# Turned orders and group releases of four-part tiles in a sparse four-layer graph network kernel

## The chip, the cores and the metric

One core of a Trainium2 chip runs the kernel. The metric is the device time of one execution in microseconds (us), lower is better; the median of several executions is compared. Engines are named as in the profile: PE multiplies matrices (PEld loads its weights), DVE and ACT work on whole tiles, POOL issues the indirect gathers, SP issues the plain DMAs.

## The reference, cut to what matters

`N` is 4096 nodes, 128 features each; `adj` is a 4096 x 4096 matrix that is mostly zero and dense in its first rows and columns. Four layers, each with a residual:

```python
h = relu(layernorm(x)); x = x + h @ W_self.T + (adj @ h) @ W_neigh.T + b                     # layer 0
h = relu(layernorm(x)); T1 = adj @ h; T2 = 2 * adj @ T1 - h
x = x + h @ w[0] + T1 @ w[1] + T2 @ w[2] + bias                                              # layer 1
h = relu(layernorm(x)); H = h @ weight.T
Tau = adj.T * exp(leaky_relu(alpha_src[None, :] + alpha_dst[:, None]))
x = x + (adj.T * Tau / Tau.sum(1)) @ H                                                       # layer 2
h = relu(layernorm(x)); s = h @ msg_s.T; d = h @ msg_d.T
agg = einsum('ijd,ij->id', gelu(s[:, None] + d[None] + msg_b), adj)                          # layer 3
x = x + layernorm(gelu([h, agg] @ upd_w.T + upd_b) + h) * ln_w + ln_b
```

## The kernel before

**What is computed where.** The kernel reads the whole of `adj` once, finds its non-zero places on the way, and from then on works on dense blocks where `adj` is dense and on lists where it is not. A list entry is a row of a feature table that POOL gathers by an indirect DMA: 128 rows at a time, one row for each partition. All gathers go through one helper, so all have the line L553 in the profile; they are told apart by their tiles.

**Three propagations (class `Layer`).** They are `adj @ h` of layer 0, and `adj @ h` and `adj @ T1` of layer 1. The output is cut into 16 stripes of 256 columns. For each stripe PE adds up the near blocks (L1138, tiles `big`, loaded by SP) and then the list chunks (L1155). A chunk takes a gathered table row tile `g` (slots `rows_g`, 14 of them) and a segment of `adj`; layer 0 gathers the segment too (`rseg`, 8 slots) and keeps it in the DRAM table `r_tab`, the others load it from there, up to four chunks in one `big` tile. Each propagation has 68 chunks. In the kernel before, the slot of a `g` tile is given back after its own matmul (L1157).

**Attention (class `Attention`, layer 2).** Per stripe of 256 columns there are batches of up to four blocks or chunks. For a batch, ACT makes `e` (relu with the gathered `g` or resident `hB` as bias, L1228, one instruction a part; exp over the batch, L1231), DVE multiplies it with the segments twice (`tau`, L1235, and `e`, L1237), and PE adds up one row of sums (L1252) and 128 rows of features (L1254), one matmul a part. 74 chunks are gathered from `a_tab` into the same 14 slots. When a pair of stripes is through, `finish_3` normalises, transposes (L588), multiplies (L597) and stores four blocks of `d_tab` (SP, L1307).

**Messages (class `Messages`, layer 3).** 158 chunks of single entries. For each, POOL gathers rows of `d_tab` into one part of a tile `m` of four parts (`m0` to `m3`, and later halves of the old `e` and `tau` tiles, which keep these names in the profile), DVE builds one part of `r` (L1400), PE adds the rows (L1406, L1408), ACT applies gelu (L1412) and PE adds up (L1418). All but 21 of these chunks need the whole of `d_tab`, and so the end of the attention; the 21 of block 0 need its first stripes alone. The value of each entry is gathered too: 158 gathers `e_val`, which only the messages need and which are put between other gathers from 500 us on.

**What sets the order.** Every piece of work is a generator that yields what it wants next: an event, a slot of a pool, or time on an engine. A planner (`Plan.run`) records the instructions in the order in which its own costs let them begin, and `in_order` pins that order on every engine. `plan.release(slots, item, time)` puts a slot back with the time from which the planner holds it free; a task that wants a slot takes the one with the smallest (time, index). So a change in a release moves which slot a later gather gets, and when the planner lets it begin, and through that the order in POOL's queue. Where the planner sees PE idle, `fill` (L604 to L609) records matmuls of zeros.

Waits are not written by hand. The build gives an instruction a wait for each earlier use of its tiles that earlier waits of its engine do not already cover, and lets an instruction of PE raise PE's semaphore only if another instruction waits for just that one (the others are counted in with the next). Where an instruction needs several waits, the further ones stand before it in its queue as instructions of their own (EventSemaphore).

`to_features` (L582 to L592) turns four blocks of 128 rows into columns: ACT has written them one by one (L578), PE transposes each into a quarter of a bank (L588), ACT copies the bank.

Of the kernel before, what the change touches and what calls it, by code (L numbers as in the profile page):

```python
# [31 lines left out]
GB = BANK // D  # L32
# [338 lines left out]
def on_pe(n, count=1):  # L371
    return "PE", (0.12 + 2.15e-3 * n) * count
# [6 lines left out]
def sparse_stack(tc, x, adj, adjT, diag, w_self, w_neigh, b0, w1, b1, w2, att_src, att_dst,  # L379
# [8 lines left out]
    plan = Plan()  # L388
    EARLY = 7
    with ExitStack() as ctx:  # L390
# [4 lines left out]
        def tiles(pool, name, n, shape, dtype=F32):  # L395
            return Slots([pool.tile(list(shape), dtype, name=f"{name}{i}", tag=f"{name}{i}") for i in range(n)])
# [20 lines left out]
        banks = tiles(ps, "bank", 3, (P, BANK))  # L417
        picks = tiles(ps, "pick", 2, (P, BANK))
# [163 lines left out]
        def to_features(blocks, rows):  # L582

            n = blocks.stop - blocks.start
            p = yield banks
            yield "PE", 0.42 * n
            for k in range(n):
                nc.tensor.transpose(p[:, k * P:(k + 1) * P], rows[:, k, :], ident)  # L588
            yield on_act(n * P)
            nc.scalar.copy(hT[:, blocks.start * P:blocks.stop * P], p[:, :n * P])  # L590
            plan.release(banks, p)
# [11 lines left out]

        def fill(begin, time):  # L604

            idle = min((free, i, slots.items) for slots in (banks, picks) for free, i in slots.free + [(1e9, 0)])
            if idle[0] < begin - 1.0:
                for _ in range(int(time / 0.22)):
                    nc.tensor.matmul(idle[2][idle[1]], nothing[:, :P], nothing, start=True, stop=True)  # L609
# [455 lines left out]
        class Layer:  # L1065
# [58 lines left out]
            def multiply(self):  # L1124
                for g in range(NC):
                    bank = yield accs
                    for s in ROWS:
                        if s.lo // BANK != g:
                            continue
                        acc = bank[:, s.lo % BANK:s.lo % BANK + RS]  # L1130
                        count, every = 0, len(s.near) + s.cap
                        for i, blocks in enumerate(s.tiles(TOGETHER)):
                            yield self.near_here[s.index][i]
                            t = self.at["near", s.index, i]
                            for k, b in enumerate(blocks):
                                yield self.near_done[b // GB]
                                yield on_pe(RS)
                                nc.tensor.matmul(acc, self.near[:, b, :D], as_rows(t)[:, k, :], start=count == 0,  # L1138
                                                 stop=count == every - 1)
                                count += 1  # L1140
                            plan.release(bigs, t)
                        for i, chunks in enumerate(s.groups(TOGETHER)):
                            if self.number:
                                yield self.list_here[s.index][i]
                                t = self.at["list", s.index, i]
                            for k, c in enumerate(chunks):
                                yield self.rows_here[s.index][c]
                                row = self.at["row", s.index, c]
                                if self.number:
                                    r = as_rows(t)[:, k, :]  # L1150
                                else:
                                    r, here, left = self.at["seg", s.index, c]
                                    yield here
                                yield on_pe(RS)
                                nc.tensor.matmul(acc, row[:, :D], r, start=count == 0, stop=count == every - 1)  # L1155
                                count += 1
                                plan.release(rows_g, row)  # L1157
                                if not self.number:
                                    left.set(plan.finish)
                            if self.number:  # L1160
                                plan.release(bigs, t)
                    agg = yield aggs
                    yield on_act(BANK)
                    nc.scalar.copy(agg, bank)
                    plan.release(accs, bank)
                    plan.start(self.finish(g, agg), -5)
                self.through.set(plan.finish)
# [6 lines left out]
        class Attention:  # L1174
# [40 lines left out]
            def attend(self, s, a, here, blocks, chunks, rows):  # L1215
                n = len(blocks or chunks)
                yield dst_done[s.lo // BANK]
                e = yield es_
                parts = []
                for k in range(n):  # L1220
                    if blocks:
                        yield a_done[blocks[k] // GB]
                        h = hB[:, blocks[k], :]
                    else:
                        yield rows[k][1]
                        h = rows[k][0]
                    yield on_act(CS + 100)
                    nc.scalar.activation(e[:, k, :], dst[:, s.lo:s.lo + CS], AF.Relu, bias=h[:, D:D + 1])  # L1228
                    parts.append(h)
                yield on_act(n * CS, "exp")  # L1230
                nc.scalar.activation(e[:, :n, :], e[:, :n, :], AF.Exp, scale=0.8)  # L1231
                yield here
                tau = yield taus
                yield on_dve(n * CS)
                nc.vector.tensor_mul(tau[:, :n, :], e[:, :n, :], a[:, :n, :])  # L1235
                yield on_dve(n * CS)
                nc.vector.tensor_mul(e[:, :n, :], tau[:, :n, :], a[:, :n, :])  # L1237
                plan.release(bigs, a)
                if s.index not in self.accs:
                    self.accs[s.index] = None  # L1240
                    self.accs[s.index] = yield accs
                    self.count[s.index] = 0
                while self.accs[s.index] is None:
                    yield acc_here[s.index]
                acc_here[s.index].set(0.0)
                every = len(s.near) + s.cap
                acc = self.accs[s.index]
                yield "PE", 0.4 * (self.count[s.index] == 0) + 2 * n * 0.65
                if self.count[s.index] == 0:
                    open_bank(acc)  # L1250
                for k in range(n):
                    nc.tensor.matmul(acc[0:1, CS:2 * CS], parts[k][:, D + 1:], tau[:, k, :], start=False, stop=False)  # L1252
                for k in range(n):
                    nc.tensor.matmul(acc[:, :CS], parts[k][:, :D], e[:, k, :], start=False,  # L1254
                                     stop=self.count[s.index] == every - 1)
                    self.count[s.index] += 1
                plan.release(taus, tau)
                plan.release(es_, e)
                for g, _ in rows:
                    plan.release(rows_g, g)  # L1260
                if self.count[s.index] == every:
                    plan.start(finish_3(s, acc), -5)
                    self.through.set(plan.finish)
# [52 lines left out]
        class Messages:  # L1316
# [27 lines left out]
            def rows(self, u, chunks, m, here):  # L1344
                groups = -(-4 * u.cuts[-1] // BANK)
                for g in range(groups):
                    yield d_here[g]
                for q, k in enumerate(chunks):
                    yield GATHER
                    n = u.within(k)  # L1350
                    gather(m[:n, q, :], d_tab[:groups * BANK, :], e_col[:n, k:k + 1])
                    here[q].set(plan.transfer(P * D * 4))

            def prepare(self, g):
# [21 lines left out]
                nc.scalar.activation(own, own, AF.Gelu)  # L1376
                r = yield r_tiles
                yield on_dve(BANK)
                for k in range(GB):
                    nc.vector.tensor_scalar(r[:, k, :], ident, diag_sb[:, g * GB + k:g * GB + k + 1], None, op0=ALU.mult)  # L1380
                self.acc[g] = acc = yield (accs if g else picks)
                yield "PE", 4 * 0.42
# [8 lines left out]
            def message(self, g, b, u, c, chunks, m, here):  # L1391
                n = len(chunks)
# [3 lines left out]
                yield self.s_here[g]  # L1396
                r = yield r_tiles
                yield "DVE", 0.35 * n
                for q, k in enumerate(chunks):
                    nc.vector.tensor_scalar(r[:, q, :], iota_row[:, :P], e_row[:, k:k + 1], e_val[:, k:k + 1],  # L1400
                                            op0=ALU.is_equal, op1=ALU.mult)
                for q in range(n):
# [91 lines left out]
        rows_g = tiles(main, "g", 14, (P, D + 2))  # L1494
# [55 lines left out]
        for i in range(2):  # L1550
# [6 lines left out]
            n = max(sum(u.cap for u in g.units) for g in GROUPS)  # L1557
# [429 lines left out]
```

## Time and profile before

| | |
|---|---|
| median of 8 runs | 1194.75 us (1189.5 to 1199.63) |
| the profiled execution | 1198.8 us, its span 1196.7 us |
| PE busy | 982.5 us, 82%, mean granted clock 0.927 |
| DVE / ACT / POOL busy | 793.9 / 672.4 / 772.4 us (66 / 56 / 65%) |
| DMA moved | 236.03 MB, mean 197 GB/s |
| gathers on POOL (L553) | 736: 68 `rseg`, 3 x 68 and 74 `g`, 74 `cseg`, 158 `e_val`, 158 of `d_tab` |
| matmuls of zeros (L609) | 795 |

PE's busy share holds the matmuls of zeros, so it does not say how much PE is needed. POOL's busy time is that of the gather instructions alone; the timeline has to be read to see at what pace they can follow each other. In lists of instructions the number in brackets is the idle time of the engine before the instruction, and what ended it. The chain of work that ended last is spread over all engines: PE 32%, DMA 28%, DVE 11%, POOL 10%, ACT 9%, issue 9%.

### The profile page before, as it was taken

What the parts mean: (1) busy time and instruction counts of PE and PEld (TensorE: products, weight loads), DVE (VectorE), ACT (ScalarE), POOL (GpSimd) and SP (SyncE); (2) the same over time, 40 slices, a digit from 0 to 9 for tenths busy, and PEclk for the clock granted to TensorE, in tenths of its full rate; (3) what the DMA queues carried; (4) which work ended last, traced back from release to release, by engine and by line L of the source; (5) the groups of instructions that cost most, each with busy time, mean ns of one, the idle gap of its engine ahead of it and who ended that gap; (6) DMA issues with size and microseconds to landing.
All of it is one profiled execution on the core that took longest, in us unless ns stands there. A gap on an engine that the chain in (4) does not pass through costs nothing.

```text
span 1196.7 us, 19187 instructions
## 1 busy us (share of the span) xinstructions
PE 982.5 (82%) x5943; PEld 672.7 (56%) x5943; DVE 793.9 (66%) x2982; ACT 672.4 (56%) x1344; POOL 772.4 (65%) x832
## 2 busy tenths in 40 slices
PE   5877988888888878778889788999999997879860
PEld 2545665555546656567667544454545665657650
DVE  5789987778878868667678665554546643356652
ACT  4997666676523221233456675686869742455771
POOL 5115777435656777777777777777777747777720
PEclk9989988879989999998899999999989999999995
DMA  7999999989748878889766533343444312223210
GB/s 225 364 329 352 388 367 394 369 305 353 262 141 268 253 222 278 249 282 288 211 192 188 171 91 106 115 116 113 111 129 122 92 51 60 52 68 86 69 36 21
DMA packets 175415, 236.03 MB, mean 197 GB/s; under 512 B 22452, under 2 KB 155336, under 8 KB 167112
## 3 DMA queue, kind: packets, MB, share of 16 engines
q1 hardware_dynamic: 148904, 186.45, 46.1%
q0 software_dynamic: 26400, 48.27, 15.7%
q8 instruction: 49, 0.80, 0.3%
q14 instruction: 62, 0.51, 0.1%
HBM read 203.41 MB, written 31.23 MB: 196 GB/s over the span
## 4 chain that ended last, share of the span: by engine, by line
PE 32%; DMA 28%; DVE 11%; POOL 10%; ACT 9%; issue 9%; SPq 1%; POOLq 0%; ACTq 0%; DVEq 0%
DMA g<-h_tab,fetch_row 5%; PE acc L1138 4%; POOL e_val L553 4%; PE acc L1155 4%; PE acc L1252 3%; PE acc L1254 3%; PE pick L609 3%; DMA big<-in_adjT 3%; DMA cseg<-in_adj,seg_col 3%; POOL g L553 3%; PE bank L609 3%; DMA dst<-in_adj 2%; PE bank L597 2%; DMA big<-r_tab 2%; DMA g<-a_tab,fetch_col 2%
## 5 line engine op out<-in xcount | busy, mean ns | idle before, releaser
L553 POOL DMA_INDIRECT e_val<-in_adj,e_at x158 | 160.0, 1013 | 48.0 <-issue 39.5
L553 POOL DMA_INDIRECT g<-h_tab,fetch_row x136 | 134.5, 989 | 45.4 <-issue 27.3
L609 PE MATMUL pick<-nothing 128*128 128x512 f16 x532 | 138.7, 409 | 0.0
L609 PEld LDWEIGHTS <-nothing 128*128 128x128 f16 x795 | 81.6, 105 | 90.8 <-issue 22.4
L1138 PE MATMUL acc<-big,hA 128*128 128x256 f32 x448 | 121.8, 418 | 12.8 <-DMA big<-in_adjT 10.0
L553 POOL DMA_INDIRECT rseg<-in_adjT,seg_row x68 | 70.7, 1039 | 77.3 <-issue 43.5
L1138 PEld LDWEIGHTS acc<-big,hA 128*128 128x128 f32 x448 | 89.7, 209 | 27.4 <-DMA big<-in_adjT 11.1
L768 ACT ACTIVATE mask<-dst 128x2048 fp8e4<-128x2048 f32 x43 | 81.9, 1905 | 25.7 <-DMA dst<-in_adj 25.5
L553 POOL DMA_INDIRECT cseg<-in_adj,seg_col x74 | 71.4, 965 | 36.6 <-issue 17.3
L553 POOL DMA_INDIRECT g<-a_tab,fetch_col x74 | 76.9, 1039 | 22.6 <-issue 13.1
L553 POOL DMA_INDIRECT m<-d_tab,e_col x70 | 68.5, 979 | 21.3 <-issue 11.6
L553 POOL DMA_INDIRECT tau<-d_tab,e_col x63 | 61.9, 983 | 30.2 <-DMA d_tab<-agg 11.3
L1155 PE MATMUL acc<-big,g 128*128 128x256 f32 x272 | 72.5, 399 | 10.2 <-DMA big<-r_tab 6.2
L1235 DVE TENSOR_TENSOR tau<-e,big 128x512 f32<-128x512 f32 (+3 forms) x61 | 54.3, 890 | 37.4 <-ACT e L1231 35.3
L553 POOL DMA_INDIRECT g<-u_tab,fetch_row x68 | 64.7, 952 | 20.7 <-issue 12.5
L568 ACT ACTIVATE junk<-xN,stat 128x128 f32<-128x128 f32 x128 | 51.3, 401 | 39.0 <-DVE stat L564 27.1
L1138 PE MATMUL acc<-big,hB 128*128 128x256 f32 x224 | 61.6, 412 | 13.4 <-DMA big<-in_adjT 13.4
L887 ACT COPY ehit<-pick 128x192 f32<-128x192 f32 (+7 forms) x74 | 20.2, 288 | 86.4 <-PE pick L884 73.3
L609 PE MATMUL bank<-nothing 128*128 128x512 f16 x263 | 66.7, 395 | 0.0
L1155 PEld LDWEIGHTS acc<-big,g 128*128 128x128 f32 x272 | 50.3, 197 | 21.7 <-issue 7.7
L890 DVE SCALAR_TENSOR_TENSOR ehit<-ehit,pos,pick 128x32 f32<-128x32 f32 (+7 forms) x158 | 38.7, 285 | 35.0 <-ACT ehit L887 34.7
L1155 PE MATMUL acc<-rseg,g 128*128 128x256 f32 x136 | 46.7, 451 | 16.6 <-DMA g<-h_tab,fetch_row 16.6
(328 smaller groups left out, 2582.0 us busy)
## 6 DMA issues: line engine op xcount, KB each, us to landing
dst<-in_adj SPq DMA_DIRECT2D x43, 1024.0 KB
big<-in_adjT SPq DMA_DIRECT2D x45, 512.0 KB
raw<-in_adj SPq DMA_DIRECT2D x21, 1024.0 KB
big<-in_adjT SPq DMA_DIRECT2D x66, 256.0 KB
big<-r_tab SPq DMA_DIRECT2D x30, 512.0 KB
c_tab<-cseg SPq DMA_DIRECT2D x74, 128.0 KB
r_tab<-rseg SPq DMA_DIRECT2D x68, 128.0 KB
big<-c_tab SPq DMA_DIRECT2D x15, 512.0 KB
```

What stands on the lines that cost most here:

```text
L553: nc.gpsimd.indirect_dma_start(out=dst, out_offset=None, in_=table[:, :], in_offset=bass.IndirectOffsetOnAxis(ap=index, axis=0))
L568: nc.scalar.activation(junk, src[:, k, :], AF.Square, bias=st[:, 0, k:k + 1], accum_out=st[:, 1, k:k + 1])
L597: nc.tensor.matmul(p[:, k * D:(k + 1) * D], lhs[:, k * P:(k + 1) * P], w, start=i == 0, stop=i == len(terms) - 1)
L609: nc.tensor.matmul(idle[2][idle[1]], nothing[:, :P], nothing, start=True, stop=True)
L768: nc.scalar.activation(mask[:, h * HALF:(h + 1) * HALF], raw_of[b, h], AF.Sigmoid, scale=1e38, accum_out=marks[:, 2 * b + h:2 * b + h + 1] ...
L887: nc.scalar.copy(hit, pv[:, :, :W])
L890: nc.vector.scalar_tensor_tensor(hit[:, q, :], hit[:, q, :], pos0[:, k + q:k + q + 1], pv[:, q, W:2 * W], op0=ALU.is_le, op1=ALU.mult, acc ...
L1138: nc.tensor.matmul(acc, self.near[:, b, :D], as_rows(t)[:, k, :], start=count == 0, stop=count == every - 1)
L1155: nc.tensor.matmul(acc, row[:, :D], r, start=count == 0, stop=count == every - 1)
L1235: nc.vector.tensor_mul(tau[:, :n, :], e[:, :n, :], a[:, :n, :])
L1252: nc.tensor.matmul(acc[0:1, CS:2 * CS], parts[k][:, D + 1:], tau[:, k, :], start=False, stop=False)
L1254: nc.tensor.matmul(acc[:, :CS], parts[k][:, :D], e[:, k, :], start=False, stop=self.count[s.index] == every - 1)
```

## The change

Six places, no instruction of the computation added or removed:

1. `to_features` transposes the four blocks last to first.
2. `Layer.multiply` gives the `g` slots of a group of up to four chunks back together after the group's last matmul, with times a millionth of a microsecond apart so that the last chunk's slot is taken first.
3. `Attention.attend` issues its sum matmuls and its feature matmuls last part first, and gives the `g` slots back with times turned in the same way.
4. `Messages.rows` gathers the parts of a tile last to first.
5. `Messages.prepare` and `Messages.message` build the parts of `r` last to first; the matmuls that read them (L1385, L1418) keep their order.
6. `fill` compares slots by time and index alone.

```diff
-            for k in range(n):
+            for k in reversed(range(n)):
                 nc.tensor.transpose(p[:, k * P:(k + 1) * P], rows[:, k, :], ident)
...
-            idle = min((free, i, slots.items) for slots in (banks, picks) for free, i in slots.free + [(1e9, 0)])
+            idle = min(((free, i, slots.items) for slots in (banks, picks) for free, i in slots.free + [(1e9, 0)]),
+                       key=lambda slot: slot[:2])
...
                                 nc.tensor.matmul(acc, row[:, :D], r, start=count == 0, stop=count == every - 1)
                                 count += 1
-                                plan.release(rows_g, row)
                                 if not self.number:
                                     left.set(plan.finish)
+                            for k, c in enumerate(reversed(chunks)):
+                                plan.release(rows_g, self.at["row", s.index, c], plan.finish + 1e-6 * k)
...
-                for k in range(n):
+                for k in reversed(range(n)):
                     nc.tensor.matmul(acc[0:1, CS:2 * CS], parts[k][:, D + 1:], tau[:, k, :], start=False, stop=False)
-                for k in range(n):
+                for k in reversed(range(n)):
                     nc.tensor.matmul(acc[:, :CS], parts[k][:, :D], e[:, k, :], start=False,
...
-                for g, _ in rows:
-                    plan.release(rows_g, g)
+                for k, (g, _) in enumerate(rows):
+                    plan.release(rows_g, g, plan.finish + 1e-6 * k)
...
-                for q, k in enumerate(chunks):
+                for q, k in reversed(list(enumerate(chunks))):
                     yield GATHER
...
-                for k in range(GB):
+                for k in reversed(range(GB)):
                     nc.vector.tensor_scalar(r[:, k, :], ident, diag_sb[:, g * GB + k:g * GB + k + 1], None, op0=ALU.mult)
...
-                for q, k in enumerate(chunks):
+                for q, k in reversed(list(enumerate(chunks))):
                     nc.vector.tensor_scalar(r[:, q, :], iota_row[:, :P], e_row[:, k:k + 1], e_val[:, k:k + 1],
```

Counted in the two built programs:

| | before | after |
|---|---|---|
| instructions of PE that raise its semaphore | 1178 | 855 |
| waits of POOL for PE | 356 | 161 |
| EventSemaphore instructions in POOL's queue | 478 | 325 |
| waits of PE for ACT / for DVE | 400 / 439 | 287 / 380 |
| waits of DVE for PE | 344 | 231 |
| matmuls of zeros (L609) | 795 | 837 |
| place of the last gather from `a_tab` among POOL's 736 gathers | 581 | 588 |
| gathers from `d_tab` that stand before it | 3 | 10 |

Up to about 390 us (the first gathers of layer 1) all engines have the same order in both builds but for the turned groups; after the last attention batch they have it again.

## The prediction

> **What bounds the kernel now.** I read the 40 slices first, then the table by stretches, POOL's waits, and last the timelines around 945 us.
>
> ```profile
> POOL 5115777435656777777777777777777747777720
> DMA  7999999989748878889766533343444312223210
> 600.00:700.00 100.00, 85.63 (x505) 64.87 (x504) 72.03 (x397) 61.02 (x149) 75.90 (x80) 0.97 0.59 173
> 800.00:900.00 100.00, 91.84 (x385) 49.33 (x383) 48.11 (x100) 74.14 (x153) 77.14 (x75) 0.91 0.39 111
> ```
>
> The first two rows are slices of 29.9 us. DMA is full up to about 300 us, while `adj` is read. POOL then stands at 7 in nearly every slice from 390 to 1140 us. The stretch rows show what that 7 means: 80 gathers in 100 us, one each 1.25 us, and a gather is busy for 0.95 of it. So from 390 us on POOL works at its own pace, and the end is set by its number of gathers, by the places where it stands still, and by a tail of some 50 us after its last gather (1146 us).
>
> ```profile
> POOL g L553 <- issue: 52.9, 175, 0.3
> POOL g L553 <- PE acc L1138: 5.2, 17, 0.3
> POOL g L553 <- PE acc L1155: 4.9, 16, 0.3
> POOL tau L553 <- DMA d_tab<-agg: 11.3, 1, 11.3
> ```
>
> These are POOL's waits: total, times, longest. The gap before a gather is 0.3 us whether PE is named as its releaser or nothing is, so waits for PE's semaphore hold POOL up nowhere after 390 us. The one true stop is the last row: 11.3 us until the last of `d_tab` has landed.
>
> ```profile
> 932.19 0.96 POOL L553 DMA_INDIRECT g<-a_tab,fetch_col  x1 [0.30 <-ACT e L1228]
> ...
> 936.04 0.95 POOL L553 DMA_INDIRECT g<-a_tab,fetch_col  x1 [0.30 <-issue]
> 937.29 0.95 POOL L553 DMA_INDIRECT m<-d_tab,e_col  x1 [0.30 <-issue]
> ...
> 958.73 0.93 POOL L553 DMA_INDIRECT e<-d_tab,e_col  x1 [0.31 <-ACT junk L568]
> 970.93 0.95 POOL L553 DMA_INDIRECT tau<-d_tab,e_col  x1 [11.27 <-DMA d_tab<-agg]
> ```
>
> The last attention gather starts at 936.04 us. POOL fills the time with the 18 early message gathers that it still has, and stops. At 970.93 it goes on with the other 137, one each 1.25 us: this moment (call it the turn) sets the end, 1196.7 - 970.9 = 225.8 us later, and that second part has the same order in both builds.
>
> **The change part by part.**
>
> *The order in POOL's queue.* The last `a_tab` gather is number 588 of 736, it was number 581: seven early message gathers now stand ahead of it. POOL is full in that stretch, so it starts 7 x 1.25 = 8.8 us later, at 944.8. How much of this reaches the turn, ACT's timeline tells:
>
> ```profile
> 935.02 0.51 ACT L1228 ACTIVATE e<-dst,g 128x256 f32<-128x256 f32 x1 [2.45 <-DMA g<-a_tab,fetch_col]
> ...
> 939.88 1.64 ACT L578 ACTIVATE hA<-xN,stat 128x128 f32<-128x128 f32 x4
> 941.44 1.29 ACT L1228 ACTIVATE e<-dst,g 128x256 f32<-128x256 f32 x3
> 942.74 1.28 ACT L1231 ACT_TABLE_LOAD   x1
> 944.04 1.06 ACT L1231 ACTIVATE e<-e 128x1024 f32<-128x1024 f32 x1
> ```
>
> The batch's first gather started at 932.19 and was used at 935.02, so a gather lands 2.83 us after it starts; the last one landed at 938.9. ACT was then busy with a norm and used it only in the run of three that ends at 942.7. In the new order that norm stands before the whole batch and ends at 941.5 as before, ahead of the last landing at 944.8 + 2.8 = 947.6; the last relu ends 0.5 later, at 948.1. That is 5.4 us later than 942.7. Table load, exp, DVE's two products, PE's eight matmuls and `finish_3` follow in the same order as before, so the turn moves by 5.4 us. Bounds: 0 if something else led that chain, 8.8 if ACT's norm is still in the way. POOL's stop grows by the same 5.4, to about 16.4: the seven gathers that were done early are missing there.
>
> *Slots of `g` given back by fours.* A gather now waits for the group's last matmul, three matmuls later than before. In the chain eight passes of L1155, which are four matmuls, take 1.97 us, 0.49 each: 1.5 us for each group that waits at all. The rows above show waits for PE that end in time, and the build has moved `e_val` gathers ahead of the groups; I take 0.5 us in all. Bounds 0 and 12: the 33 waits that name PE are some 8 groups, each 1.5. In the attention the semaphore times of the trace show PE done with a slot 5 us and more before a gather takes it, so nothing there.
>
> The Trainium skill, "Perfetto Trace Analysis", section Optimization Strategy, speaks against this part: a gap that repeats on the engine that should be saturated can mean that there is not enough SBUF for the next tile, and slots held longer act like fewer slots. By that rule the 12 would be the value; by the 0.3 us rows it is near 0.
>
> *PE's semaphore, 323 raises fewer.* Two groups of equal matmuls, of which the first rarely raises it (53 of 158 matmuls of L1408) and the second nearly always (151 of 158 of L1418):
>
> ```profile
> 955.36 1.05 PE L1408 MATMUL bank<-s,msel 128*128 128x128 f32 x8
> 967.88 1.06 PE L1418 MATMUL pick<-r,e 128*128 128x128 f32 x8
> ```
>
> 0.01 us on four matmuls: 323 raises are worth at most 323 x 0.01 / 4 = 0.8 us of PE, and PE does not bound after 390 us. Taken as 0, bounds -0.8 and 0. "TensorE: Matmul & The Clock Gate", section The cost: per-tile semaphore tail, gives 26.3 ns for each increment of concurrent tiles; by it the sum would be -8.5 us if all lay on the path, by the two rows it is nothing.
>
> *153 EventSemaphores fewer on POOL.* In the build the gather at 936.04 has three waits and the one at 937.29 a single one: they start 1.26 and 1.25 us after the gather before them (the first of these started at 934.78). The waits are worked off under the gather before. 0; the lower bound is 153 x 0.01 = -1.5 us.
>
> *Turned reads.* PE's transposes now begin after the fourth relu: three of them, 3 x 0.15 us (four took 0.59 in the chain), are no longer hidden. On the way to the turn the copy behind them waited for ACT's gelu anyway (965.23 to 965.70): 0, bounds 0 and 0.45. The turned `r` parts and message gathers lie under POOL's pace (78 gathers between 1000 and 1100 us, PE busy 79% and DVE 47%). In the tail, where DVE's queue of `r` parts is on the chain, the first part waits for a matmul up to 3 x 0.26 us later (1.06 / 4, L1418): 0.2, bounds 0 and 0.8.
>
> *42 more matmuls of zeros*, 0.22 us each (48 took 10.36), 9 us of PE in the layers and the attention, where PE has such matmuls because it idles: 0, bound 2.
>
> Sum against the profiled execution: 5.4 + 0.5 + 0.2 = 6.1, span 1202.8, its time 1198.8 + 6.1 = 1204.9. That execution is 4.05 above the median, so I move the median: 1194.75 + 6.1 = 1200.9, 1201 us, +0.5%. 0.5% (6 us) is about what a measurement of this kernel can tell from no change.
>
> **The rivals.**
>
> *Hidden.* The turn is led by PE or DVE, not by the last gather. For it: PE's matmuls run without idle time from 943 to 951 us, DVE has 4.2 us of memsets in that chain. Against: ACT waited 2.45 us for the batch's first gather. Then 0 to 2 us remain: 1196.
>
> *Faster.* From 700 to 930 us POOL makes 75 to 77 gathers in 100 us, not 80: three to five times 1.25 us lost in each, some 10 us in all. If that loss is POOL's work on waits, the 153 that go win it back: -10, and with the later turn's 5.4 still paid -4.6; with that hidden as well 1185. Between them: 1189. It decides if the mean distance of gathers in the attention falls from 1.33 to 1.27 or less. Against: in the layers, where waits are as dense, the stretch row shows the full 80.
>
> *Starved.* The groups' slots come late in both last propagations: the 12 us bound in place of 0.5, 1194.75 + 5.4 + 0.2 + 12 = 1212. It would need POOL gaps of 1 us and more before groups of `g` between 400 and 680 us.
>
> That the change does not do what it says is ruled out by the counts of the build.
>
> **How the numbers follow.** Forecast 0.50 (own range 1197 to 1206; its middle is at the border, and its bounds reach further up: 0.34 of it slower, 0.16 same), hidden 0.13 (same), faster 0.19 (0.18 faster, 0.01 same), starved 0.18 (slower). Faster 0.18, same 0.30, slower 0.52. The range holds the first two and half of each of the others, which leaves out 0.09 on either side: 1189, the middle of the faster rival, to 1210, since starving may be partial.
>
> **What would show it.** Right: the last `a_tab` gather near 945 us, the turn near 976, POOL's stop there near 16 us instead of 11.3, 225 us from the turn to the end, gathers still 1.25 us apart. Wrong: the last gather at 936 or earlier (POOL got faster), the turn unmoved with the gather late (hidden), gaps before groups of `g` between 400 and 680 us (starved), or a distance from the turn to the end that differs from 225.8 by more than 2 us, which I have no term for.

## The result and the profile after

| | before | after |
|---|---|---|
| median | 1195.58 us (33 runs, 1189.5 to 1202.19) | 1204.52 us (12 runs, 1198.52 to 1206.93) |
| ratio, 95% interval | 1 | 1.0070 (1.0053 to 1.0087) |
| the profiled execution, its span | 1198.8, 1196.7 us | 1205.71, 1203.8 us |
| first gather of the messages after POOL's stop (the turn) | 970.93 us | 978.33 us |
| turn to the end | 225.7 us | 225.5 us |

The change makes the kernel 0.7% slower. In the two profiles all of it lies ahead of the turn. The lines of the page after that answer to those shown of before:

```profile
span 1203.8 us, 19136 instructions
PE 987.8 (82%) x5985; PEld 674.2 (56%) x5985; DVE 790.9 (66%) x2982; ACT 672.4 (56%) x1344; POOL 769.3 (64%) x832
POOL 5115777355366777777777778777777637777720
DMA  7999999999659788898765433343444312223200
```

Busy times hardly moved (PE +5.3 us for 42 matmuls of zeros more). The same table by stretches as before, and POOL's waits (total, times, longest):

```profile
600.00:700.00 100.00, 79.11 (x449) 60.66 (x447) 66.00 (x380) 57.44 (x138) 75.62 (x81) 0.90 0.57 162
800.00:900.00 100.00, 93.98 (x426) 50.60 (x426) 52.28 (x111) 76.81 (x163) 76.84 (x77) 1.00 0.41 115
```

```profile
POOL g L553 <- issue: 63.9, 211, 0.3
POOL tau L553 <- DMA d_tab<-agg: 15.2, 1, 15.2
POOL e L553 <- ACT mt L623: 6.8, 2, 6.5
POOL g L553 <- PE acc L1156: 2.1, 7, 0.3
```

POOL makes 81 gathers in 100 us in the layers (80 before) and 77 in the attention (75 before), and a gather of `g` waits for PE nowhere longer than 0.3 us. What grew is its idle time at the end of the attention, in two pieces, 6.5 and 15.2 us instead of one of 11.3. POOL's timeline shows where:

```profile
941.72 0.94 POOL L553 DMA_INDIRECT g<-a_tab,fetch_col  x1 [0.30 <-issue]
942.97 0.94 POOL L553 DMA_INDIRECT m<-d_tab,e_col  x1 [0.30 <-issue]
...
954.18 0.94 POOL L553 DMA_INDIRECT e<-d_tab,e_col  x1 [6.54 <-ACT mt L623]
...
978.33 0.94 POOL L553 DMA_INDIRECT tau<-d_tab,e_col  x1 [15.15 <-DMA d_tab<-agg]
```

The last `a_tab` gather is number 588, as the build says. ACT's timeline shows whether anything waits for it:

```profile
943.24 1.65 ACT L578 ACTIVATE hA<-xN,stat 128x128 f32<-128x128 f32 x4
944.79 1.29 ACT L1230 ACTIVATE e<-dst,g 128x256 f32<-128x256 f32 x3
946.93 0.58 ACT L590 COPY hT<-bank 128x512 f32<-128x512 f32 x1 [0.85 <-PE bank L588]
947.41 0.51 ACT L1230 ACTIVATE e<-dst,g 128x256 f32<-128x256 f32 x1
947.94 1.28 ACT L1233 ACT_TABLE_LOAD   x1
949.24 1.06 ACT L1233 ACTIVATE e<-e 128x1024 f32<-128x1024 f32 x1
```

Its landing (941.72 + 2.83 = 944.55, if it lands as fast as before) is not what the last relu at 947.41 waited for: a norm and a copy stand ahead of it on ACT, and the idle time before them names PE, not a DMA. Exp is at 949.24, 5.2 us later than before, though the last gather isn't on its path. So the whole sequence of batches was already late. The last store of `d_tab`, which the turn waits for, is issued 5.7 us later; before, then after:

```profile
968.02 0.36 SPq L1307 DMA_DIRECT2D d_tab<-agg  x1
```

```profile
973.73 0.36 SPq L1309 DMA_DIRECT2D d_tab<-agg  x1
```

From there to the turn it is 2.91 us before and 4.60 after: 1.7 us of the turn's 7.4 come in this last step, behind everything that the change orders.

### The profile page after: what moved, and what is told of

It is laid out like the page before. It is cut to its first block, busy times and chain, and to the rows that moved or that the text cites. A ratio compares the mean times of both kernels' runs of the same rounds, so it can differ in the third digit from the quotient of the medians.

```text
span 1203.8 us, 19136 instructions
## 1 busy us (share of the span) xinstructions
PE 987.8 (82%) x5985; PEld 674.2 (56%) x5985; DVE 790.9 (66%) x2982; ACT 672.4 (56%) x1344; POOL 769.3 (64%) x832
## 4 chain that ended last, share of the span: by engine, by line
DMA 28%; PE 19%; POOL 16%; DVE 13%; ACT 12%; issue 10%; SPq 1%; POOLq 0%; DVEq 0%; ACTq 0%
POOL g L553 4%; POOL e_val L553 4%; DMA g<-h_tab,fetch_row 4%; DMA e_val<-in_adj,e_at 3%; DMA cseg<-in_adj,seg_col 3%; PE pick L610 3%; DMA dst<-in_adj 3%; ACT mask L769 2%; DMA g<-a_tab,fetch_col 2%; DMA m<-d_tab,e_col 2%; POOL tau L553 2%; PE acc L1156 2%; ACT junk L568 2%; PE bank L597 2%; PE acc L1139 2%
## 5 line engine op out<-in xcount | busy, mean ns | idle before, releaser
L610 PE MATMUL pick<-nothing 128*128 128x512 f16 x563 | 143.5, 403 | 0.0
L610 PEld LDWEIGHTS <-nothing 128*128 128x128 f16 x837 | 85.5, 104 | 96.0 <-issue 23.1
L1139 PE MATMUL acc<-big,hA 128*128 128x256 f32 x448 | 118.4, 406 | 6.9 <-DMA big<-in_adjT 3.7
L1139 PEld LDWEIGHTS acc<-big,hA 128*128 128x128 f32 x448 | 85.4, 201 | 19.8 <-DMA big<-in_adjT 5.1
L1156 PE MATMUL acc<-big,g 128*128 128x256 f32 x272 | 76.6, 418 | 13.3 <-DMA big<-r_tab 7.9
L553 POOL DMA_INDIRECT tau<-d_tab,e_col x63 | 61.2, 971 | 34.0 <-DMA d_tab<-agg 15.2
L610 PE MATMUL bank<-nothing 128*128 128x512 f16 x274 | 72.5, 407 | 0.0
L888 ACT COPY ehit<-pick 128x192 f32<-128x192 f32 (+9 forms) x74 | 20.1, 286 | 85.2 <-PE pick L885 70.9
L1156 PEld LDWEIGHTS acc<-big,g 128*128 128x128 f32 x272 | 53.2, 207 | 25.8 <-DMA g<-h_tab,fetch_row 8.8
L623 ACT ACTIVATE sel_t<-iota_row,mids 128x512 f32<-128x512 f32 (+3 forms) x43 | 27.1, 641 | 60.4 <-DVE mids L618 53.0
```

The lines of the kernel that those rows point to most:

```text
L553: nc.gpsimd.indirect_dma_start(out=dst, out_offset=None, in_=table[:, :], in_offset=bass.IndirectOffsetOnAxis(ap=index, axis=0))
L623: nc.scalar.activation(lane["t"][:, :n * P], iota_row[:, :n * P], AF.Abs, bias=mids[:, g:g + 1])
L888: nc.scalar.copy(hit, pv[:, :, :W])
```

## Experiments

The front of the kernel varies from one execution to the next: the 141st gather starts between 348.0 and 355.2 us in the profiles below (the first four runs apart). I therefore measure from the 441st gather, near the start of the attention, to the turn, both from POOL's timeline; "mean place" is how many places further back in POOL's queue the 74 `a_tab` gathers stand than in the kernel before, on average, counted in the traces.

| run | change in it | last `a_tab` | mean place | 441st to turn | turn to end | median | ratio to before (95%) |
|---|---|---|---|---|---|---|---|
| before | none | 581 | 0 | 223.1 | 225.7 | 1195.58 | 1 |
| after | all | 588 | +5.5 | 232.4 | 225.5 | 1204.52 | 1.0070 (1.0053 to 1.0087) |
| e2_group_only | release by fours in the layers | 588 | +5.5 | 232.0 | 225.6 | 1205.85 | 1.0079 (1.0047 to 1.0111) |
| e2_all_but_group | all but that | 581 | 0 | 222.3 | 226.5 | 1196.13 | 0.9990 (0.9958 to 1.0022) |
| e2_hold_early | all, `d_tab` gathers held | 578 | +4.9 | 230.4 | 233.0 | 1209.24 | 1.0119 (1.0083 to 1.0155) |
| e2_rows_first | all but that, rows first | 563 | -13.8 | 211.0 | 231.6 | 1191.07 | 0.9967 (0.9944 to 0.9990) |
| e3_all_paced | all, queue as before | 579 | -1.2 | 222.3 | 223.9 | 1189.67 | 0.9935 (0.9909 to 0.9960) |
| e3_before_eager | none, queue as after | 587 | +5.5 | 228.8 | 228.3 | 1204.05 | 1.0047 (1.0028 to 1.0065) |
| e3_late_valid | all, DVE's `e_val` later | 588 | +5.6 | 230.9 | 224.6 | 1200.78 | 1.0018 (0.9998 to 1.0038) |
| e3_rows_first_tail | rows first, end mended | 563 | -13.8 | 212.1 | 231.8 | 1196.37 | 0.9992 (0.9969 to 1.0014) |

The kernel before took 1196.15 us beside the e2 runs and 1197.98 beside the e3 runs; the ratios are within a group. There is one profile of each kernel, so a distance is that of a single execution.

The time from the issue of the last store of `d_tab` to the turn is 2.9 us in before, group_only, all_but_group, hold_early, all_paced and before_eager, also where the profile names DVE as what the turn waited for, but 4.60 in the kernel after and 4.95 in late_valid. No run shows why. From the 441st gather to the issue of this store it is 220.2 us before, 227.8 after, 229.1 in group_only, 219.4 in all_but_group, 227.5 in hold_early, 219.4 in all_paced, 225.9 in before_eager and 225.9 in late_valid.

**The first four, on a chip that answers nothing.** The first four kernels (all shown below, as e2) ran on a chip on which the kernel before took 1560.7 us too.

> Only the release of the g buffers by fours in the two first layers, on the kernel before (with the filler's comparison of times alone, which it needs). Nothing else of the change is in it: all reads and writes keep their old order, and 1150 of the kernel's 1178 raises of PE's semaphore stay. In the instructions as built the last gather from a_tab is number 588 on POOL, as in the kernel after, instead of 581. Order theory (the place of that gather sets the turn, 1.25 us a place, and the rest of the change is worth little): the whole +8.9 us is here, ratio 1.005 to 1.009, 1202 to 1207 us, the last a_tab gather near 942 to 946 and the first tau gather near 976 to 980. Turned-reads theory (what starts only when the last of four parts has landed loses time): about the kernel before, ratio 0.998 to 1.002. Slots theory (g buffers that come free later hold up POOL's gathers of the two first layers): as slow as after, but with the front late already before 700 us.

> The kernel after without the release by fours in the two first layers: every turned read and write, the attention's releases in turned order, and 881 raises of PE's semaphore instead of 1178. The last a_tab gather is number 581, as before. Order theory: as the kernel before, ratio 0.998 to 1.003 (1193 to 1199 us), first tau gather near 969 to 972, so that 297 raises fewer are worth nothing either way. Turned-reads theory: ratio 1.005 to 1.009, the turn late by 5 to 8 us with the last a_tab gather in time. [...]

> The kernel after, and the gathers from d_tab of the messages' first stretch are not asked for until the last gather from a_tab stands in the queue: that one is number 578 instead of 588, and no d_tab gather is ahead of it (10 in the kernel after, 3 in the kernel before). All of the change stays in, the release by fours too. Order theory: 10 places of 1.25 us are 12.5 us; the turn comes that much earlier than after's 978.3 as far as POOL's remaining gathers ahead of the turn fill its time: between 966 and 971, so 1190 to 1196 us, ratio 0.995 to 1.001. Turned-reads and Slots theories: the order at the turn doesn't matter, about the kernel after, ratio 1.004 to 1.009.

> The kernel after without the release by fours, and the attention's row gathers are asked for ahead of the wait for a tile of their scores, so that the last a_tab gather is number 563 (581 in the kernel before), no d_tab gather ahead of it. The arithmetic is the same. Order theory carried on: 18 places of 1.25 us are 22.5 us of POOL's queue, but only the 11.3 us that POOL stood idle at the turn before can be had from it, since its whole load of gathers stays: 1184 to 1190 us, ratio 0.990 to 0.996, and POOL's stop at the turn under 5 us. If what the norm of the last blocks waits for is not the row gather but the scores behind it (ACT and DVE are in the way), the turn stays near 970 and the ratio near 1.000. Turned-reads theory: as the kernel after or a little above, 1.005 to 1.010.

Measured: 1539.15 us, 0.9884 (0.9843 to 0.9925); 1548.06 us, without an interval; 1543.04 us, 0.9875 (0.9818 to 0.9933); 1529.52 us, 0.9811 (0.9759 to 0.9862). Two of the waits of e1_group_only (total, times, longest):

```profile
ACT sel_t L623 <- issue: 44.6, 4, 25.1
PE bank L597 <- issue: 41.6, 14, 24.4
```

"issue" is idle time for which the profile has no reason; in the kernels before and after, no such wait of these two lines is among the 200 largest groups of waits, which go down to 0.7 and 0.6 us. There the last `a_tab` gather of e1_group_only started at 1180.63 and the turn came 52.5 us later (36.6 in the kernel after). Engines stood still elsewhere, the queue's order did not set the turn, and the expectations could not be told apart. The four were run again.

**Which part of the change.** The edit of group_only against the kernel before:

```diff
-                                plan.release(rows_g, row)
...
+                            for k, c in enumerate(reversed(chunks)):
+                                plan.release(rows_g, self.at["row", s.index, c], plan.finish + 1e-6 * k)
```

(with `fill`'s key). all_but_group is the kernel after with this edit undone.

> The kernel of e1_group_only again (the release of the g buffers by fours in the two first layers alone), since all kernels of that call, the kernel before among them, took some 1540 us on that chip, with engines standing still for 5 to 40 us where no wait shows, so that the queue of POOL didn't set the turn there. On a chip on which the kernel before takes about 1195 us, Order theory: the whole +8.9 us is here, ratio 1.005 to 1.009, first tau gather near 976 to 980. Turned-reads theory: ratio 0.998 to 1.002. Slots theory: as slow as after, late already before 700 us.

> The kernel of e1_all_but_group again (the kernel after without the release by fours in the two first layers). Order theory: ratio 0.998 to 1.003, first tau gather near 969 to 972. Turned-reads theory: ratio 1.005 to 1.009. [...]

Measured: 1.0079 and 0.9990, as the Order theory expected; the turns are 0.4 and 1.3 us later than its limits, less than the front varies by. POOL's timeline at the turn, first group_only, then all_but_group:

```profile
944.13 0.95 POOL L553 DMA_INDIRECT g<-a_tab,fetch_col  x1 [0.30 <-DVE tau L1237]
...
980.40 0.95 POOL L553 DMA_INDIRECT tau<-d_tab,e_col  x1 [12.53 <-DMA d_tab<-agg]
```

```profile
938.81 1.42 POOL L553 DMA_INDIRECT g<-a_tab,fetch_col  x1 [0.30 <-ACT junk L568]
...
973.32 0.95 POOL L553 DMA_INDIRECT tau<-d_tab,e_col  x1 [9.99 <-DVE r L1401]
```

The release by fours in the layers carries the loss, and the other five edits with 297 raises fewer carry none that can be seen. The layers show no loss of this size: from the 161st to the 401st gather it is 305.8 us in group_only and 305.4 before. This stretch varies by more than the half microsecond that I had put down for the slots, 307.5 in the kernel after and 309.5 in all_but_group, which has no release by fours, so it rules out the 12 us and not 0.5 or 2. The Turned-reads and Slots theories fall here.

**Is it the last gather's place?** hold_early, against the kernel after (`attention.asked` counts the `a_tab` gathers put into the queue):

```diff
             def rows(self, u, chunks, m, here):
+                if u.block == 0:
+                    yield attention.asked
                 groups = -(-4 * u.cuts[-1] // BANK)
```

> The kernel of e1_hold_early again (the kernel after, with the d_tab gathers of the first stretch held until the last a_tab gather stands in the queue: number 578 instead of 588). Order theory: first tau gather between 966 and 971, ratio 0.995 to 1.001. Turned-reads and Slots theories: about the kernel after, ratio 1.004 to 1.009.

Measured: 1.0119, a miss. The last `a_tab` gather, ACT, and the turn:

```profile
929.40 1.39 POOL L553 DMA_INDIRECT g<-a_tab,fetch_col  x1 [0.30 <-ACT hT L590]
```

```profile
944.86 1.65 ACT L578 ACTIVATE hA<-xN,stat 128x128 f32<-128x128 f32 x4
946.41 1.29 ACT L1232 ACTIVATE e<-dst,g 128x256 f32<-128x256 f32 x3
```

```profile
976.38 0.94 POOL L553 DMA_INDIRECT tau<-d_tab,e_col  x1 [11.99 <-DVE own L1380]
```

The last gather lies 17 us ahead of the relus that read that batch, and the distance to the turn fell by 2.0 us (232.4 to 230.4), not by 12. Of these 2.0 us, 1.7 are the last store's way to the turn; to its issue it is 0.2 us. So the Order theory is wrong as I had put it: the place of the last gather sets next to nothing here. Besides, this kernel's end is 7.5 us longer (233.0 to 225.5): the planner has put the last messages' gelu on ACT behind a norm of the output. I took that for the cause of the longer end and tested it below.

**All rows earlier.** rows_first, against all_but_group: a task of its own asks for the attention's rows, ahead of the wait for a tile of scores.

```diff
+            def ahead(self):
+                for number, (s, blocks, chunks) in enumerate(self.units()):
+                    if not chunks:
+                        continue
...
+                    for c in chunks:
+                        g = yield rows_g
+                        rows.append((g, Event()))
...
+                    yield from self.rows(s, chunks, rows)
```

> The kernel of e1_rows_first again (no release by fours, the attention's row gathers asked for ahead of the wait for a tile of scores: last a_tab gather number 563 instead of the kernel before's 581). Order theory carried on: 0.990 to 0.996, POOL's stop at the turn under 5 us. If the scores (ACT and DVE) are what the last norm waits for, not the row gather, the turn stays near 970, POOL's stop grows, and the ratio is near 1.000. Turned-reads theory: 1.005 to 1.010. On the chip of the first call this kernel was 1.9% under the kernel before.

Measured: 0.9967 (0.9944 to 0.9990), just above the expected range. The turn comes 11.3 us earlier than in all_but_group (211.0 to 222.3), as expected, POOL's stop there is 1.35 us, and then 5.1 us go again at the end. ACT's waits for rows in before, after and rows_first:

```profile
ACT e L1228 <- DMA g<-a_tab,fetch_col: 41.1, 21, 12.2
```

```profile
ACT e L1230 <- DMA g<-a_tab,fetch_col: 42.6, 26, 10.1
```

```profile
ACT e L1241 <- DMA g<-a_tab,fetch_col: 6.5, 7, 1.6
```

In both the kernel before and the kernel after ACT waits some 42 us for gathered rows, all through the attention. This is what led to the next theory: each `a_tab` gather counts, and in the kernel after each stands 2 to 9 places further back, behind `e_val` gathers (the last eight wholly or in part behind `d_tab` gathers). POOL's gathers of `e_val` in three stretches (start and end, length, busy time and number of them), before and after:

```profile
500.00:740.00 240.00, 87.78 (x89) 0.94 0.65 196
740.00:800.00 60.00, 19.32 (x19) 0.97 0.44 127
...
920.00:960.00 40.00, 4.44 (x4) 1.00 0.31 84
```

```profile
500.00:740.00 240.00, 89.01 (x91) 0.93 0.65 193
740.00:800.00 60.00, 23.20 (x21) 0.91 0.41 118
...
920.00:960.00 40.00, 0.00 (x0) 1.00 0.37 101
```

The 158 values, which only the messages need, are all fetched before 920 us in the kernel after. In this theory the attention's rows pay for it.

**The queue by itself, both ways.** all_paced is the kernel after plus waits in the planner that keep `e_val` gathers behind the `a_tab` gathers that stood ahead of them before (`ROWS_AHEAD` is the list of their numbers); before_eager is the kernel before with the reverse list.

```diff
                     for k in range(u.chunk, u.chunk + u.cap):
+                        if ROWS_AHEAD[asked["v"]]:
+                            yield a_asked[ROWS_AHEAD[asked["v"]] - 1]
                         yield GATHER
...
+                if u.block == 0:
+                    yield a_asked[69]
                 groups = -(-4 * u.cuts[-1] // BANK)
```

```diff
                 for c, (g, here) in zip(chunks, rows):
+                    yield v_asked[VALUES_AHEAD[asked["a"]] - 1]
                     yield GATHER
```

> The kernel after with all of its change, and POOL's queue in the attention put back to the kernel before's: an e_val gather isn't asked for until as many a_tab gathers stand in the queue as stood ahead of it in the kernel before, and the first stretch's d_tab gathers not until 70 do. The 74 a_tab gathers then stand at the kernel before's numbers or up to two ahead of them (436 to 579; 436 to 581 there, 439 to 588 in the kernel after). e2_hold_early moved the last ten of them alone, and its turn came only 2 to 3 us earlier. Queue-throughout theory (what counts is the place of every a_tab gather in the attention, behind 3 to 9 more e_val gathers in the kernel after, not of the last one): 0.997 to 1.002 of the kernel before, 1193 to 1198 us, turn near 970. Layers theory (the later releases delay the end of the second layer on PE and DVE, and the queue only shows it): 1.004 to 1.009.

> The kernel before with nothing of the change in it, and POOL's queue put into the kernel after's order: an a_tab gather isn't asked for until as many e_val gathers stand in the queue as stood ahead of it in the kernel after. The a_tab gathers stand at 439 to 587 (439 to 588 in the kernel after), nine d_tab gathers ahead of the last. 1173 raises of PE's semaphore, all releases one by one. Queue-throughout theory: the whole loss without any of the change, 1.005 to 1.010, turn near 977 to 980. Layers theory: as the kernel before, 0.998 to 1.002.

Measured: 0.9935 and 1.0047. The turn in all_paced, then in before_eager:

```profile
966.16 0.94 POOL L553 DMA_INDIRECT tau<-d_tab,e_col  x1 [8.77 <-DVE r L1417]
```

```profile
975.98 0.95 POOL L553 DMA_INDIRECT tau<-d_tab,e_col  x1 [12.54 <-DMA d_tab<-agg]
```

With the whole change in it, but the queue of before, the distance to the turn is 222.3 us, 10.1 less than after and like before's 223.1. With nothing of the change in it, but the queue of after, it is 228.8, 5.7 more than before, and the kernel is 0.47% slower (0.28 to 0.65): ratio and turn both lie a little below what the Queue-throughout theory expected, and outside what the Layers theory did. This shows that the loss comes through the order in the attention that POOL's queue leads, and not through the layers; the orders of ACT, DVE and PE follow the planner's queue in both kernels, so queue and followers are not separated. One follower is a rival of its own, the matmuls of zeros on PE: between 740 and 940 us there are 61 of them before and in all_but_group and 66 in all_paced, but 90 in the kernel after and in group_only and 99 in before_eager, 6 to 9 us of PE more. The planner adds them where it sees PE idle, so they can be an effect of the later rows as well as a cause of the loss; no run changes them alone. The order gives 5.7 of the 9.3 us without any of the change. Of the other 3.6 in the kernel after, 1.7 are the last store's way to the turn; the rest is not shown, nor are 3.2 of group_only's 8.9 us up to that store. all_paced is below its expected range and faster than both kernels. Of its 6.7 us against the profile of before, 4.0 lie ahead of the 441st gather (743.8 to 747.8), where the front varies by as much anyway, 0.8 up to the turn and 1.8 after it; why it is faster than the kernel before, and not merely as fast, stays open.

**DVE's waits.** DVE also multiplies `e_val`, in its own order, and waits there for these gathers to land. late_valid puts that multiplication later in the kernel after:

```diff
-                        valued[u.number].set(plan.finish + plan.LANDING)
+                        valued[u.number].set(plan.finish + plan.LANDING + 6.0)
```

> The kernel after, POOL's queue unchanged (a_tab gathers at 439 to 588), but DVE's multiplication of e_val stands some 6 us later in DVE's order, so that it needn't wait there for its gather to land. DVE waited for such landings 66.0 us in 20 waits in the kernel after, 48.4 in 15 in the kernel before. Theory that the e_val gathers cost through DVE's waits for them rather than through their places in POOL's queue: these waits fall under 25 us, and the attention gets back most of what it lost, 0.995 to 1.003. Queue-throughout theory: DVE's waits fall as well, but DVE is then early for what the a_tab gathers set, and the time stays, 1.004 to 1.009.

Measured: 1.0018. The waits of DVE and ACT in the kernel after, then in late_valid:

```profile
DVE e_val L946 <- DMA e_val<-in_adj,e_at: 66.0, 20, 7.8
...
ACT e L1230 <- DMA g<-a_tab,fetch_col: 42.6, 26, 10.1
```

```profile
DVE e_val L946 <- DMA e_val<-in_adj,e_at: 23.3, 9, 4.3
...
ACT e L1230 <- DMA g<-a_tab,fetch_col: 49.3, 31, 15.0
```

The ratio is the one that the DVE theory expected; the trace is not. 42.7 us of DVE's waits are gone, ACT's waits for rows grew by 6.7, and the distance to the turn fell by 1.5 us of 9.3. In this profile the attention got back little of its time: 1.5 us, or 1.8 up to the last store. Nor do DVE's waits go with the distance in the other runs: they are 60.8 us in all_paced and 59.3 in all_but_group, which lost nothing, and 52.9 in before_eager, which did. But the ratios of the runs, 1.0018 against 1.0070, say that more than half of the loss was won back. Where the rest of it is from, these runs don't tell (2.5 us lie ahead of the 441st gather in the profiles and 0.9 behind the turn), and a part of the loss that goes through these waits is not ruled out.

**The longer end.** rows_first_tail is rows_first with one more wait: the norm of the last output stretch but one begins only when the last messages' gelu stands in ACT's order.

```diff
+                if g == NC - 2:
+                    yield self.spoken
                 st = yield stats
```

> The kernel of e2_rows_first, whose turn came 13 us earlier relative to its front but which gave 6 us back at the end, where the last messages' gelu stood on ACT behind the norm of the last stretch but one: here that norm is not begun until the last gelu stands in ACT's order, as it does in the kernels before and after. POOL's queue is that of e2_rows_first (a_tab gathers at 427 to 563). Expected: the turn near 957 to 960, the stretch from the turn to the end 225 to 227 instead of 231.7, so 1183 to 1188 us, ratio 0.989 to 0.994. If the longer end was not ACT's order, it stays near 0.997.

Measured: 0.9992, turn to end 231.8 instead of the 225 to 227 expected: a miss. The turn is as early as in rows_first, the end as long. The hold brought the last gelu nearer to the turn, 188.8 us behind it instead of 193.4 (184.1 in the kernel after), but the norm that it held came 6.2 us later. So putting ACT's order right in this one place does not give the time back; the cause of the longer end is open.

## Why the prediction was right, and where it was not

- **POOL's pace and the second part.** POOL bounds from 390 us on at 1.25 us a gather; the turn sets the end 225.8 us later. Measured 225.5: right.
- **The term of 5.4 us.** It was mis-sized, and its reason was wrong. The step that failed is "In the new order that norm stands before the whole batch and ends at 941.5 as before". It ended 3.3 us later (943.24 + 4 parts, next instruction 944.79), since everything ahead of it was late as well. The gather itself started at 941.72 and not at 944.8. The turn moved by 7.4 us on the clock and by 9.3 us from the 441st gather, 1.7 of them between the last store and the turn. I had looked at the last of the 74 gathers, because the last wait was there, and counted seven places (that `e_val` gathers move ahead I had seen, but priced in the layers alone); hold_early shows that ten places of that gather are worth 0.2 us up to the last store. In its place: the `a_tab` gathers stand 2 to 9 places back all through the attention, 5.5 on average, and all_paced and before_eager show that this order, with what follows it on the other engines, moves the turn. 5.5 places of 1.25 us are 6.9 us, and the seven places of the last gather, less what ACT's norm hid, were 5.4: that the two lie close together is luck, and it is why the forecast held.
- **Slots by fours, 0.5 us.** Not contradicted: 305.8 us in the layers in group_only against 305.4 before, but 307.5 in the kernel after, in a stretch that varies by as much without the edit. The bound of 12 us was not reached. By the rule on too little SBUF in the Trainium skill ("Perfetto Trace Analysis", Optimization Strategy) it would have been the value; the gap that repeats, which this rule goes by, is not in POOL's rows.
- **Raises of PE's semaphore, 0.** Right within what can be seen: all_but_group, with 297 raises fewer, is at 0.9990 (0.9958 to 1.0022). The skill's "TensorE: Matmul & The Clock Gate", The cost: per-tile semaphore tail, would make 297 x 26.3 ns = 7.8 us if all of them lay on the path, an estimate that means 0.9935; the interval excludes that, and no run shows what a raise costs by itself.
- **Turned reads, EventSemaphores, zeros: 0 to 0.4.** Turned reads and EventSemaphores: not seen in all_but_group. The zeros are not in it; 29 more than before stand between 740 and 940 us, and what they cost is open.
- **POOL's stop of 16.4 us.** By my own terms it would be 11.3 + 5.4 = 16.7. It became 15.2 at the turn, and a second one of 6.5 before it that I had no term for: an early message gather waited, by the profile, for ACT.
- **Rivals.** Hidden: the last gather was indeed hidden, but the turn moved. Faster needed the mean distance of gathers in the attention to fall from 1.33 to 1.27; from the 437th to the 586th gather it is 1.34 in both. Starved needed gaps of 1 us and more before groups of `g` between 400 and 680 us; there is one, 1.68 us at 475 us, which the profile puts down to a DMA and not to a slot.

Sum 6.1 us against 8.9 measured (ratio 1.0053 to 1.0087, so 6.3 to 10.4 us): inside the range of the forecast, by one term that was too small and reasoned from the wrong gather. What was right is that the loss comes through the order in POOL's queue and shows ahead of the turn; that the sum came as near as it did is partly luck.

## What to carry to other kernels

Where a planner sets the order, an edit of when buffers come free is an edit of a queue's order somewhere else: compare the place of every member of the sequence that matters, not of its last one, before costing it. A wait at the end of a chain shows only what came last there; move that one thing alone, and if the time does not follow, look for what made the rest of the chain late. Work that nobody needs yet (here the values for the messages) should be kept behind work that somebody waits for: with the old order of the queue the same change was 0.65% faster than the kernel before instead of 0.7% slower, though why it is faster than before stays open.

## What the runs showed of the hardware

On one chip the same program took 1560.7 us instead of 1196, at a granted clock of 0.82 instead of 0.92. In e1_group_only, at a clock of 0.835, POOL's gathers there still took 0.94 us and mostly followed each other at 1.25, but ACT and PE stood still for up to 25 us at a time, and DVE once for 34, with no wait in the profile. I have no cause for it. On such a chip a question of 0.7% in a queue's order can't be asked.
